# Two attention layers in fp32 on one core: the value products leave PSUM by VectorE instead of ScalarE

## Chip, cores and metric

The kernel runs on one core of one Trainium2 chip. The metric is the device time of one execution in microseconds (us).

## What is computed

The input is four images of 32 x 32 positions and 768 channels, in fp32. Two layers follow each other. Each normalises its input over 32 groups of channels, computes attention over the 1024 positions of an image with 12 heads of 64 channels and a relative position bias in both directions, projects the result and adds it to the layer's input. Cut to what matters here:

```
qkv    = groupnorm(x) @ Wqkv (+ qkv_b, in layer 1 only)
scores = scale * q @ k.T + rel_h[..., :, None] + rel_w[..., None, :]
attn   = softmax(scores)
out    = attn @ v                      # the value products
x      = x + (out @ Wproj + bproj)
```

The bias of the values can be added after the softmax, because the weights of one query sum to one. The kernel does this: in layer 1 the step that takes the value products out of PSUM adds the values' part of `qkv_b`.

## The kernel before

There are eight images in the sense of the code (`images`): four in layer 0, then the same four in layer 1. An image has six pairs of heads (`pair`), so there are 48 groups `g`, and each group has eight units `n` of 128 queries (`units`). The order of all instructions is written out by hand in the main loop, and each engine works through its own queue in that order.

In unit (g, n) the loop issues, in this order:

- on GpSimd, the position biases of the unit after next (`biases`, L429);
- on TensorE, the scores of the next unit (`scores`, L443) into two PSUM tiles `s`; on VectorE, the sum of scores and bias with its row minimum (L455), and on ScalarE the exponentials (L459) (`exponentials`);
- at n = 7, on TensorE, the position products of the next group (`positions`, L381) into a PSUM tile `tp`, which ScalarE copies out (L386, L389); at n = 2 another half of them;
- parts of the projections of other groups (`products`, tile `pj`; `project_values`, tile `pv`; `project_out_two`, tile `oo`), whose matmuls are recorded at L285 and L313. Such a group of matmuls is split in two halves. Between the halves VectorE rewrites one column of a weight tile with its own value (L274, `between`), so that the second half waits for it;
- on VectorE, the transpose of the unit's weights (`turn`, L479) into a tile `tb`, of which there are two; then a DMA writes `tb` to a scratch tensor `td` in DRAM, and another one reads it back in the order that the value products need, into `pt` (L490);
- the division of the next unit's weights by their sums (`divide`): a reciprocal on VectorE (L467), and two multiplications on ScalarE (L473), one of which is on GpSimd (L471) where n is 2 or 4;
- at n = 6 the value products of the first two quarters of the group's queries, and at n = 2 those of the last two quarters of the group before (`weigh`, L508): 64 matmul records into one PSUM tile `av` of 128 x 512, followed by one instruction that writes it to the tile `attn` in SBUF (L517 in layer 0, a plain copy; L519 in layer 1, a copy with the bias `bqkv`). The last group's last two quarters are done apart, in two instructions of 128 x 256.

The tiles `tp`, `pj`, `pv`, `oo`, `o` and `av` share one PSUM pool, `ps_m`, with two buffers. The next of them can start on TensorE only when the buffer that it gets has been read out:

```
ps_s = ctx.enter_context(tc.tile_pool(name="ps_s", bufs=2, space=PSUM))
ps_m = ctx.enter_context(tc.tile_pool(name="ps_m", bufs=2, space=PSUM))
```

At the change from n = 6 to n = 7, one of the two buffers holds the half-finished group `oo` and the other one holds `av`. What TensorE has next after the scores is `tp`, which gets the buffer of `av`.

The image's normalisation is prepared while the image before is still worked on: its statistics and their square root in pair 3, and its application on ScalarE (L233, `apply`) in pair 4.

Of the kernel before, what the change touches and what calls it, by code (L numbers as in the profile page):

```python
# [32 lines left out]
AF = mybir.ActivationFunctionType  # L33
ALU = mybir.AluOpType
# [22 lines left out]
def attention_blocks(ctx: ExitStack, tc: tile.TileContext, a: dict, out: bass.AP):  # L57
    nc = tc.nc
# [115 lines left out]
    bqkv = const.tile([P, 3, NP], FP, tag="bqkv", name="bqkv")  # L174
# [320 lines left out]
    def weigh(g, quarters):  # L495

        if quarters[0] == 0:  # L500
            attn_of[g] = apool.tile([P, S], FP, tag="attn", name=f"attn_{g}")
        n = len(quarters)
        av = ps_m.tile([P, S], FP, tag="m", name=f"av_{g}_{quarters[0]}")[:, : n * 2 * P]
        for at, quarter in enumerate(quarters):
            for k in range(NT):
                for h in range(2):
                    rows = slice(h * D, (h + 1) * D)
                    nc.tensor.matmul(  # L508
                        av[rows, at * 2 * P : (at + 1) * 2 * P], lhsT=v_of[g][:, k, rows],
                        rhs=pt_of[g, quarter].rearrange("p n r k h i -> p (n r) k h i")[:, :, k, h, :],  # L510
                        start=(k == 0), stop=(k == NT - 1),
                    )
        at = quarters[0] * 2 * P
        to = attn_of[g][:, at : at + n * 2 * P]
        im, pair = divmod(g, NP)
        if images[im][0] == 0:
            nc.scalar.copy(to, av)  # L517
        else:
            nc.scalar.activation(to, av, AF.Identity, bias=bqkv[:, 2, pair : pair + 1])  # L519

    def cuts(im):
        return [0, NC // 2, NC] if im + 1 < NI else [0, NC // 2, NC - 1, NC]
# [161 lines left out]
    with tc.manual_schedule(engines=ENGINES):  # L684
# [55 lines left out]
        for at, (g, n) in enumerate(units):  # L740
            im, pair = divmod(g, NP)
# [81 lines left out]
            if n == 6:  # L823
                weigh(g, (0, 1))
            elif n == 2 and g:
                weigh(g - 1, (2, 3))
# [4 lines left out]
        for quarter in (2, 3):  # L831
            weigh(NPAIR - 1, (quarter,))
# [57 lines left out]
```

## Time and profile before

| what | value |
|---|---|
| median of 3 runs | 3404.13 us (3402.43 to 3408.83) |
| the profiled execution | 3401.86 us |
| its span | 3400.0 us |
| TensorE matmul busy | 3324.9 us, 98% of the span |
| VectorE busy | 2347.4 us, 69% |
| ScalarE busy | 2090.8 us, 61% |
| GpSimd busy | 2332.3 us, 69% |
| granted TensorE clock | 0.998 |

The span runs from the first to the last instruction of the program. PE is TensorE's matmuls, PEld its weight loads, DVE VectorE, ACT ScalarE, POOL GpSimd and SP the engine that issues most DMAs. L443 is line 443 of the kernel. In a row of waits, the part ahead of the arrow waited for the part behind it; the numbers are the total time in us, how often, and the longest one. In a timeline, a row has start and duration in us, engine, line, operation, output and inputs, how many instructions were merged, and in brackets the idle time of the engine before it and what ended it.

### The profile page before, as it was taken

What the parts mean: (1) busy time and instruction counts of PE and PEld (TensorE: products, weight loads), DVE (VectorE), ACT (ScalarE), POOL (GpSimd) and SP (SyncE); (2) the same over time, 40 slices, a digit from 0 to 9 for tenths busy, and PEclk for the clock granted to TensorE, in tenths of its full rate; (3) what the DMA queues carried; (4) which work ended last, traced back from release to release, by engine and by line L of the source; (5) the groups of instructions that cost most, each with busy time, mean ns of one, the idle gap of its engine ahead of it and who ended that gap; (6) DMA issues with size and microseconds to landing.
All of it is one profiled execution on the core that took longest, in us unless ns stands there. A gap on an engine that the chain in (4) does not pass through costs nothing.

```text
span 3400.0 us, 58086 instructions
## 1 busy us (share of the span) xinstructions
PE 3324.9 (98%) x21600; PEld 1877.2 (55%) x21600; DVE 2347.4 (69%) x3826; ACT 2090.8 (61%) x3237; POOL 2332.3 (69%) x1184
## 2 busy tenths in 40 slices
PE   6999999999999999999999999999999999999998
PEld 3555555555555555555555555555555555555554
DVE  3776677766777666766767766666766676666675
ACT  2666756566566666566665666666666667665663
POOL 5776866668666686666866668666686667766662
PEclk9999999999999999999999999999999999999999
DMA  3898989999998998889888989989988999898887
GB/s 112 307 325 300 335 298 337 321 304 327 317 318 316 318 324 309 309 297 332 313 309 311 312 311 320 317 310 315 325 314 305 332 299 335 308 311 301 312 292 259
DMA packets 534777, 1046.97 MB, mean 308 GB/s; under 512 B 149728, under 2 KB 212704, under 8 KB 485344
## 3 DMA queue, kind: packets, MB, share of 16 engines
q1 hardware_dynamic: 479936, 1015.84, 85.3%
q10 hardware_dynamic: 54560, 27.43, 2.8%
q8 instruction: 171, 2.80, 0.3%
q14 instruction: 110, 0.90, 0.1%
HBM read 568.01 MB, written 475.10 MB: 307 GB/s over the span
## 4 chain that ended last, share of the span: by engine, by line
PE 81%; DMA 7%; DVE 4%; ACT 4%; issue 2%; POOL 1%; SPq 1%; ACTq 0%; DVEq 0%; POOLq 0%
PE pj L285 20%; PE s L443 16%; PE av L508 14%; PE pv L285 13%; PE oo L285 12%; DMA td<-tb 5%; PE pj L313 3%; PE tp L381 2%; DVE tb L479 2%; ACT sc L473 2%; POOL sc L429 1%; PE o L587 1%; ACT sc L459 1%; DMA xn<-in_x 1%; ACT xn L233 1%
## 5 line engine op out<-in xcount | busy, mean ns | idle before, releaser
L429 POOL TENSOR_TENSOR sc<-rel 128x1024 f32<-128x1024 f32 x768 | 1879.7, 2476 | 660.1 <-DVE tb L479 626.8
L455 DVE CUSTOM_DVE_ANT_0 sc<-s,sc 128x1024 f32<-128x1024 f32 x768 | 910.8, 1225 | 747.9 <-PE s L443 561.9
L459 ACT ACTIVATE sc<-sc,sm 128x1024 f32<-128x1024 f32 x768 | 878.7, 1146 | 472.0 <-DVE sm L455 471.0
L473 ACT ACTIVATE sc<-sc,sm 128x1024 f32<-128x1024 f32 x674 | 743.0, 1143 | 581.2 <-DVE sm L467 415.4
L479 DVE STREAM_TRANSPOSE tb<-sc 128x1024 f32<-128x1024 f32 x768 | 909.9, 1227 | 52.8 <-DMA td<-tb 44.7
L443 PE MATMUL s<-k,q 64*128 64x512 f32 x3072 | 738.3, 596 | 1.7 <-DVE sm L455 1.7
L508 PE MATMUL av<-pt,v 128*64 128x256 f32 x6144 | 685.5, 381 | 7.0 <-DMA pt<-td 6.0
L508 PEld LDWEIGHTS av<-pt,v 128*64 128x64 f32 x6144 | 434.8, 137 | 287.0 <-issue 45.0
L285 PE MATMUL pv<-wv,xn 64*128 64x256 f32 x4608 | 522.8, 376 | 1.0 <-DVE wv L274 1.0
L285 PEld LDWEIGHTS pv<-wv,xn 64*128 64x128 f32 x4608 | 447.3, 187 | 114.1 <-issue 56.9
L285 PE MATMUL oo<-attn,wo 64*128 64x512 f32 x2112 | 477.1, 591 | 0.0
L443 PEld LDWEIGHTS s<-k,q 64*128 64x128 f32 x3072 | 290.1, 187 | 313.7 <-issue 292.2
L285 PEld LDWEIGHTS oo<-attn,wo 64*128 64x128 f32 x2112 | 202.0, 188 | 228.7 <-issue 227.2
L471 POOL TENSOR_SCALAR sc<-sc,sm 128x1024 f32<-128x1024 f32 x94 | 105.1, 1118 | 311.8 <-DVE sm L467 310.8
L285 PE MATMUL pj<-xn,wa 64*128 64x512 f32 x1152 | 269.1, 598 | 33.2 <-DVE xn L235 27.4
L285 PE MATMUL pj<-xn,w 64*128 64x512 f32 x1152 | 263.4, 589 | 1.6 <-DVE w L274 1.6
L285 PE MATMUL pj<-s,w 64*128 64x512 f32 x576 | 262.7, 589 | 1.5 <-ACT attn L519 0.8
L285 PE MATMUL pj<-s,wc 64*128 64x512 f32 x576 | 262.8, 589 | 0.0
L285 PEld LDWEIGHTS pj<-xn,wa 64*128 64x128 f32 x1152 | 113.6, 189 | 168.9 <-issue 127.4
L285 PEld LDWEIGHTS pj<-xn,w 64*128 64x128 f32 x1152 | 112.4, 187 | 136.6 <-issue 134.1
L404 ACT COPY rel<-raw 32x256 f32<-32x256 f32 x384 | 155.1, 404 | 22.2 <-DMA part<-res 6.7
L285 PEld LDWEIGHTS pj<-s,wc 64*128 64x128 f32 x576 | 107.4, 187 | 67.0 <-issue 67.0
(68 smaller groups left out, 2111.4 us busy)
## 6 DMA issues: line engine op xcount, KB each, us to landing
td<-tb SPq DMA_DIRECT2D x384, 1024.0 KB, 6.5
pt<-td SPq DMA_DIRECT2D x382, 1024.0 KB, 8.9
tdr<-t ACTq DMA_DIRECT2D x96, 256.0 KB, 6.3
part<-res SPq DMA_DIRECT2D x84, 256.0 KB, 4.5
res<-part SPq DMA_DIRECT2D x84, 256.0 KB, 4.9
wa<-in_wqk SPq DMA_DIRECT2D x48, 384.0 KB, 3.2
wc<-in_wqk SPq DMA_DIRECT2D x48, 384.0 KB, 7.4
wv<-in_wv SPq DMA_DIRECT2D x24, 768.0 KB, 12.2
```

The source lines that it names most:

```text
L285: nc.tensor.matmul(to, lhsT=w, rhs=x, start=(half, at) == (0, 0), stop=(half, at) == (1, n - 1))
L313: nc.tensor.matmul(t[:, h, :], lhsT=w[rows, c, :], rhs=x[c][rows, :], start=(c == 0), stop=(c == NB - 1),)
L381: nc.tensor.matmul(ps[:, h, j, :], lhsT=q[rows, at * P : (at + 1) * P], rhs=tabs[l][rows, :], start=True, stop=True,)
L404: nc.scalar.copy(rel[rows, :, 0, :, :], raw[rows, :, :, WIDE - 1 - HW - y : WIDE - 1 - y])
L429: nc.gpsimd.tensor_tensor(sc.rearrange("p (a k) (u l) -> p a (k u) l", a=4, l=8), rel[:, h, 0, m, :].unsqueeze(1).unsqueeze(3).to_broadcas ...
L443: nc.tensor.matmul(ps[h][:, cols], lhsT=q[rows, n * P : (n + 1) * P], rhs=k[rows, cols], start=True, stop=True,)
L455: nc.vector.tensor_tensor_reduce(out=sc, in0=ps[h], in1=sc, scale=-scale, scalar=BIG, op0=ALU.add, op1=ALU.min, accum_out=st[:, 0, h : h + 1],
L459: nc.scalar.activation(sc, sc, AF.Exp, bias=st[:, 0, h : h + 1], scale=-1.0, accum_out=st[:, 1, h : h + 1],)
L471: nc.gpsimd.tensor_scalar(sc, sc, st[:, 2, h : h + 1], 1.0, ALU.mult, ALU.mult)
L473: nc.scalar.mul(sc, sc, st[:, 2, h : h + 1])
L479: nc.vector.transpose(tb[:, :, h, :], sc_of[g, n, h])
L508: nc.tensor.matmul(av[rows, at * 2 * P : (at + 1) * 2 * P], lhsT=v_of[g][:, k, rows], rhs=pt_of[g, quarter].rearrange("p n r k h i -> p (n ...
```

## The change

The instruction that takes `av` out of PSUM goes from ScalarE to VectorE, with the same tiles and at the same place in the written order. In layer 0 it is a copy; in layer 1 it is a VectorE operation with one tensor input and one bias value per partition. There are 97 such instructions in the program (48 copies of 128 x 512, 47 with the bias of 128 x 512, and two with the bias of 128 x 256). The instructions of TensorE, GpSimd and SP and their order stay as they are.

```
@@ -514,9 +514,9 @@
         to = attn_of[g][:, at : at + n * 2 * P]
         im, pair = divmod(g, NP)
         if images[im][0] == 0:
-            nc.scalar.copy(to, av)
+            nc.vector.tensor_copy(to, av)
         else:
-            nc.scalar.activation(to, av, AF.Identity, bias=bqkv[:, 2, pair : pair + 1])
+            nc.vector.tensor_scalar(to, av, bqkv[:, 2, pair : pair + 1], None, ALU.add)
```

More of the change, by code (lines that the diff above doesn't have):

```diff
@@ L516, in weigh @@
         if images[im][0] == 0:
-            nc.scalar.copy(to, av)
+            nc.vector.tensor_copy(to, av)
         else:
-            nc.scalar.activation(to, av, AF.Identity, bias=bqkv[:, 2, pair : pair + 1])
+            nc.vector.tensor_scalar(to, av, bqkv[:, 2, pair : pair + 1], None, ALU.add)
     def cuts(im):
```

## Prediction

> **What bounds the kernel now.** I read the page's busy line first. It says TensorE, and says how little is left to win:
>
> ```profile
> PE 3324.9 (98%) x21600; PEld 1877.2 (55%) x21600; DVE 2347.4 (69%) x3826; ACT 2090.8 (61%) x3237; POOL 2332.3 (69%) x1184
> ```
>
> So the question is not how busy VectorE and ScalarE are, but where TensorE is idle: 3400.0 - 3324.9 = 75 us. The table of windows puts 27 us before 37 us (the start), 13 us up to 300, 12 us in the last 102 us, and 22.7 us in the long middle:
>
> ```profile
> 300.00:3298.00 2998.00, 2975.34 (x19536) 1.00 0.90 315
> ```
>
> (columns: window, its length, PE busy, granted clock, DMA share, GB/s). The view of waits, for PE alone, names what ends this idle time:
>
> ```profile
> PE pj L285 <- DVE xn L235: 27.4, 1, 27.4
> PE tp L381 <- ACT attn L517: 13.0, 12, 2.0
> PE tp L381 <- ACT attn L519: 7.3, 8, 2.1
> PE av L508 <- DMA pt<-td: 6.0, 6, 1.6
> PE o L587 <- ACT attn L519: 3.8, 3, 2.0
> ```
>
> The first row is the start. The next two are 20 waits, 20.3 us, and the reader is to see what they wait for: the very instruction that the change moves. `tp` needs the PSUM buffer of `av`, and TensorE stands until ScalarE has read it out.
>
> The timeline of one such place (group 27, unit 6 to 7), ScalarE's and VectorE's rows, tells why ScalarE is late:
>
> ```profile
> 1976.67 2.37 DVE L479 STREAM_TRANSPOSE tb<-sc 128x1024 f32<-128x1024 f32 x2 [3.21 <-DMA td<-tb]
> 1978.97 0.12 DVE L467 RECIPROCAL sm<-sm 128x2 f32<-128x2 f32 x1
> 1979.01 0.13 DVE L274 TENSOR_REDUCE wo<-wo 128x1 f32<-128x1 f32 x1
> 1979.99 1.22 DVE L455 CUSTOM_DVE_ANT_0 sc<-s,sc 128x1024 f32<-128x1024 f32 x1 [0.85 <-PE s L443]
> ```
> ```profile
> 1979.12 2.19 ACT L473 ACTIVATE sc<-sc,sm 128x1024 f32<-128x1024 f32 x2 [3.45 <-DVE wo L274]
> 1981.22 0.67 ACT L519 ACTIVATE attn<-av,bqkv 128x512 f32<-128x512 f32 x1
> ```
> ```profile
> 1977.86 1.99 PE L443 MATMUL s<-k,q 64*128 64x512 f32 x8
> 1981.94 0.83 PE L381 MATMUL tp<-tab,q 64*128 64x128 f32 x10 [2.09 <-ACT attn L519]
> ```
>
> `av` was complete at 1977.93. ScalarE reads it at 1981.22, because the two divisions stand ahead of it, and these wait for VectorE's reciprocal, which is late because the transposes waited for a DMA. VectorE itself idles 0.85 us before L455.
>
> [...] The trace's nearest rows agree as lower neighbours: 684 (L608, a sum of PSUM and SBUF, 128x512) and 747 ns (L606, the same with a bias). [...] So L429 on GpSimd should keep its 2476 ns; no row of before shows this instruction. [...] the rows above agree, since L519 starts right behind the divisions.
>
> **The change part by part.**
>
> *Removed from ScalarE:* 48 x 562 ns + 47 x 666 ns + 2 x 473 ns = 59 us. ScalarE is 39% idle and only its lateness counts, so this alone is worth nothing; L459 behind it starts up to 0.6 us earlier.
>
> *Added to VectorE:* 97 instructions. [...] from above 759 (L331, PSUM with bias and an SBUF input); I take 690, so 66 us, 71% busy in place of 69%. In the new order the eviction stands directly behind the next unit's reciprocal and ahead of L274 and L455. It waits for the end of `av`, so at what times do its neighbours run? I measured from the end of `av` in VectorE's timeline, at all places. L455 starts at +2.06 (2.04 at n = 2), held by the scores that TensorE does after `av`. The reciprocal ends at -2.21 at n = 2 nearly always. At n = 6 it ends at -2 to -1 in most groups without a stall, and between -0.7 and +0.65 in those with one, but for two with +1.13 and +1.16. The eviction therefore lies between max(0, reciprocal) + 0.05 and about 0.75 us later: it fits in VectorE's idle time ahead of L455. Cost on the path: nothing, hidden by the wait for the scores. Were that cover gone, 0.69 us at each of 95 places.
>
> *The stall at `tp`.* Undisturbed, `tp` starts 1.82 us after the first scores matmul (2258.21 to 2260.03); at 1977.86 it took 4.08. I summed the excess over 1.82 in all 47 groups: 23.7 us in 20 groups (0.4 to 2.3 each), 14 of them in pair 3 or 4. `tp` could start at `av` + 1.75. With the eviction ending at max(0, reciprocal) + 0.75, 18 of the 20 end by +1.40 and stall no more; the other two end at +1.9 and keep 0.2 each. Gain 23.7 - 0.4 = **23.3 us**.
>
> *Two more stalls of the kind*, `pj` at n = 3 in groups 5 and 40 (352.65 and 2853.38), where ScalarE applied the norm ahead of the eviction (+4.5 us): 0.9 each, gain **1.8 us**.
>
> *The end.* In the last group `o` waits 2.2 us at 3357.93 for an eviction at 3357.31, whose reciprocal had ended at 3355.10: with VectorE it ends near 3355.85 and **2.0 us** are won. A like wait of 1.3 us at 3329.98 is followed by waits for `pt`; I count nothing.
>
> *The wait added to VectorE.* At n = 3 L274 on `wv` (`between`) now stands behind the eviction, and the second half of `pv` waits for it. L274 ends at about +0.05 + 0.69 + 0.15 = +0.9; the first weight load of that half starts at +1.33 (2019.87). Margin 0.4 us. In groups 6 and 12 a BN_STATS of 0.68 us lies between them: loss 2 x 0.3 = **0.6 us**. SP's and GpSimd's queues are not passed by anything.
>
> *What is late next.* `pt`. The second quarter's data land 2.6 us (median) before their first matmul, but in stalled groups often only 1 us. Taking the stall of a group from the next group's margin leaves at least 0.2 us everywhere, so no wait is new in a first count. But DMA is at 0.90 of the middle window, and all of this pushes it to 2698 / 2974 = 0.91. Given back: 0 to 10 us; I take **2.5**.
>
> Sum: 23.3 + 1.8 + 2.0 - 0.6 - 2.5 = 24 us. The profiled execution of 3401.86 would become 3377.9. It lies 2.3 us under the median of the runs, 3404.13; that median less 24 is **3380**.
>
> **The rivals.** (A) *The stall turns into waits for DMA.* Lateness starts with transposes waiting for `tb` (44.7 us in 26 waits on VectorE), a DMA matter, and TensorE running earlier doesn't make DMA faster. For it: the 0.90, and six waits for `pt` that exist already. Against: groups without a stall all take 68.72 us, so DMA keeps up with a TensorE that never waits. Half to two thirds given back: 3404 - 11 = 3393.
> (B) *The change doesn't do what it says:* the buffer is not what holds `tp`, the releaser being inferred. Against: `tp` starts 0.04 to 0.05 us after ScalarE's eviction at each place that I read. No change: 3404.
> (C) *Slower: VectorE's queue holds TensorE.* With the eviction ahead of L274 and L455, a longer one delays `pv` at n = 3. The margin of 0.4 us is used up at 1.1 us of eviction; to outweigh the 27 us won, 34 us / 47 groups = 0.72 us more, that is 1.8 us an eviction. No row of 128x512 on VectorE from PSUM comes near (the slowest, strided, 1225 ns), and L274's own place is not on the path otherwise. It would give 3411.
>
> **How the numbers follow.** About 0.2% (7 us) is what a measurement of this kernel can tell from no change. My forecast has 0.73; A 0.16, of which some 0.04 ends within 0.2%; B 0.05; C 0.06. Faster: 0.73 + 0.12 = 0.85; same 0.09; slower 0.06. The range: nothing given back and the 1.3 us at the end won too is 29 us, 3375, less 3 us for the scatter of three medians; at the other end A's 3393. I give 3372 to 3394.
>
> **What would show it.** In the profile after: the rows of `tp` waiting for `attn` gone or under 1 us in all; PE idle in the middle window down from 22.7 to about 3 us; the eviction on VectorE at 0.65 to 0.76 us; L455 still at +2.06; DVE 71%, ACT 60%. The prediction is wrong if `tp` still waits (for whom, the waits tell), if PE's waits for `pt` or `wv` grow by over 10 us, or if L429 gets slower.

## The result, and the profile after

The changed kernel takes 3369.21 us in the median of four runs (3366.87 to 3373.25), the kernel before in the same set 3405.31 us (3402.43 to 3408.83): 36 us less, a ratio of 0.9898 with a 95% interval from 0.9886 to 0.9911. The prediction named 3380 us and a range of 3372 to 3394; direction and mechanism hold, the gain is larger than forecast, and the time lies 3 us under the range. Two more sets of runs of the same two kernels, made with the experiments, give 3400.09 to 3373.87 (ratio 0.993, 0.9916 to 0.9943) and 3401.18 to 3371.59 (0.991, 0.9897 to 0.9923). The gain of the three sets is 36, 26 and 30 us.

The profiled execution after took 3373.25 us, with a span of 3370.8. Busy line and the window of the middle, as they stood in the prediction:

```profile
PE 3319.2 (98%) x21600; PEld 1875.8 (56%) x21600; DVE 2415.5 (72%) x3923; ACT 2039.6 (61%) x3140; POOL 2332.4 (69%) x1184
```
```profile
300.00:3268.00 2968.00, 2966.27 (x19514) 1.00 0.91 318
```

The share of 98% says nothing new. The window does: TensorE idles 1.7 us in 2968, where it idled 22.7 in 2998. VectorE took over 68 us of work and ScalarE gave up 51. The new instruction itself, as the view of `attn` has it (shortest, median and longest in ns):

```profile
L519 DVE TENSOR_SCALAR attn<-av,bqkv x49: 483/751/752, 1754.9 to 3360.7; 128x512 f32<-128x512 f32 x47, 128x256 f32<-128x256 f32 x2
L517 DVE COPY attn<-av x48: 664/691/693, 127.6 to 1722.7; 128x512 f32<-128x512 f32 x48
```

The view of waits for PE no longer has a row in which `tp` waits for `attn`:

```profile
PE pj L285 <- DVE xn L235: 26.7, 1, 26.7
PE av L508 <- DMA pt<-td: 9.0, 6, 2.6
PE pj L285 <- DVE wa L274: 3.8, 2, 3.2
...
PE o L587 <- DVE attn L519: 0.6, 1, 0.6
```

The waits for `pt`, the weights that a DMA reads back for the value products, grew from 6.0 to 9.0 us. The timeline of the same place as before, group 27 at the change from unit 6 to 7, first VectorE, then ScalarE, then TensorE:

```profile
1959.50 2.37 DVE L479 STREAM_TRANSPOSE tb<-sc 128x1024 f32<-128x1024 f32 x2 [2.54 <-DMA td<-tb]
1961.79 0.12 DVE L467 RECIPROCAL sm<-sm 128x2 f32<-128x2 f32 x1
1961.84 0.73 DVE L519 TENSOR_SCALAR attn<-av,bqkv 128x512 f32<-128x512 f32 x1
1962.48 0.14 DVE L274 TENSOR_REDUCE wo<-wo 128x1 f32<-128x1 f32 x1
1963.08 1.23 DVE L455 CUSTOM_DVE_ANT_0 sc<-s,sc 128x1024 f32<-128x1024 f32 x1 [0.46 <-PE s L443]
```
```profile
1961.95 2.19 ACT L473 ACTIVATE sc<-sc,sm 128x1024 f32<-128x1024 f32 x2 [2.79 <-DVE sm L467]
```
```profile
1960.95 1.99 PE L443 MATMUL s<-k,q 64*128 64x512 f32 x8
1962.77 1.06 PE L381 MATMUL tp<-tab,q 64*128 64x128 f32 x16
```

The reader is to see three things. The transposes are late as before, because a DMA still holds `tb` (2.54 us of idle time here). The eviction now runs (from 1961.84) while ScalarE only begins its divisions (1961.95). And `tp` starts 1.82 us after the scores, the undisturbed distance; L455 still waits for the scores after the eviction (0.46 us).

### The profile page after: what moved, and what is told of

It reads as the page before. It is cut to its first block, busy times and chain, and to the rows that moved or that the text cites. A ratio compares the mean times of both kernels' runs of the same rounds, so it can differ in the third digit from the quotient of the medians.

```text
span 3370.8 us, 58086 instructions
## 1 busy us (share of the span) xinstructions
PE 3319.2 (98%) x21600; PEld 1875.8 (56%) x21600; DVE 2415.5 (72%) x3923; ACT 2039.6 (61%) x3140; POOL 2332.4 (69%) x1184
## 4 chain that ended last, share of the span: by engine, by line
PE 93%; DMA 4%; DVE 2%; issue 1%; ACT 0%; SPq 0%; POOL 0%; ACTq 0%; DVEq 0%
PE pj L285 21%; PE av L508 19%; PE s L443 19%; PE pv L285 15%; PE oo L285 13%; PE pj L313 3%; PE tp L381 3%; DMA td<-tb 2%; DMA pt<-td 1%; PE o L587 1%; DVE tb L479 1%; DMA xn<-in_x 0%; DVE sc L455 0%; DVE st L188 0%; DMA per<-mv 0%
## 5 line engine op out<-in xcount | busy, mean ns | idle before, releaser
L429 POOL TENSOR_TENSOR sc<-rel 128x1024 f32<-128x1024 f32 x768 | 1880.3, 2478 | 636.8 <-DVE tb L479 601.6
L455 DVE CUSTOM_DVE_ANT_0 sc<-s,sc 128x1024 f32<-128x1024 f32 x768 | 910.9, 1225 | 524.0 <-PE s L443 459.5
```

The source lines that it names most:

```text
L429: nc.gpsimd.tensor_tensor(sc.rearrange("p (a k) (u l) -> p a (k u) l", a=4, l=8), rel[:, h, 0, m, :].unsqueeze(1).unsqueeze(3).to_broadcas ...
L455: nc.vector.tensor_tensor_reduce(out=sc, in0=ps[h], in1=sc, scale=-scale, scalar=BIG, op0=ALU.add, op1=ALU.min, accum_out=st[:, 0, h : h + 1],
```

## The experiments

**The changed kernel again**, to size the gain.

> The changed kernel once more, against the kernel before, to size the gain. The first profiles give 28.6 us (3401.86 to 3373.25), the first medians 36.1. If the two profiled executions were ordinary ones, more rounds give 28 to 30 us. If the profiled execution of before was a lucky one and that of after an unlucky one (they were the lowest and the highest of their kind), more rounds give 33 to 37 us, and the new profile's span is some 5 us below 3370.8, with fewer waits of TensorE for pt (9.0 us in the first).

Measured: 3373.87 us (3370.95 to 3380.64) against 3400.09 (3392.33 to 3412.39, 19 runs), 26 us. Beside the third set:

> The changed kernel in a third set of runs, beside the kernels of this set. The two sets so far give 36 and 26 us of gain. If that is scatter between executions, the third lies between 24 and 38 and its profile again shows under 3 us of waits at tp.

Measured: 3371.59 us (3369.13 to 3371.61) against 3401.18, 30 us. The excess at `tp`, summed as in the prediction, is 0.6, 2.4 and 0.3 us in the three profiles, and PE's waits for `pt` are 9.0, 3.8 and 7.4 us. The second set's 26 us lie in neither range of its expectation (28 to 30, or 33 to 37), though the waits for `pt` did become fewer, and the new span, 3368.6, is 2.2 us below the first, not 5. The third set's 30 us lie in the range expected. The three intervals don't all overlap, so what differs from set to set is more than the scatter inside a set; its cause was not found.

**The kernel before again.**

> The kernel before in another profiled execution, to see how much its stalls scatter. If its time scatters because of them (its runs lie between 3392 and 3412 us), the sum of excess at tp differs from 23.7 by several us, or the half-clock stretches and the waits for pt do.

Measured: 3402.82 us. The excess at `tp` is 22.8 us (23.8 in the first profile), so this term is stable. What differs is the clock. After three of the stalls TensorE's granted clock was half for 3.4 us; in the first profile this followed one stall in the middle and one at the end. The windows around one of them, PE alone (columns: window, its length, busy, granted clock, DMA share, GB/s):

```profile
2464.00:2467.00 3.00, 1.64 (x8) 1.00 0.93 367
2468.00:2471.00 3.00, 3.00 (x20) 0.52 0.94 308
2472.00:2475.00 3.00, 3.00 (x16) 1.00 0.97 316
```

The stall of 1.98 us ends at 2467.6, and the clock is 0.52 in the window right after it.

**ScalarE first.** The eviction stays on ScalarE, ahead of the divisions:

```
             turn(g, n)
             run_part(1 if n == 0 else len(pieces))
+            if n == 6:
+                weigh(g, (0, 1))
+            elif n == 2 and g:
+                weigh(g - 1, (2, 3))
             if at + 1 < len(units):
                 divide(*units[at + 1])
...
-            if n == 6:
-                weigh(g, (0, 1))
-            elif n == 2 and g:
-                weigh(g - 1, (2, 3))
```

> The eviction stays on ScalarE, but is issued ahead of the two divisions instead of behind them; no other engine's order changes. Theory 1 (place in the queue): what counts is that the buffer of av is read out before tp needs it; the eviction ends near av + 0.75 or reciprocal + 0.6, tp waits under 1 us in all, and the time is that of the changed kernel within 5 us. Theory 2 (the engine): ScalarE's relief of 59 us or VectorE's free time makes the gain; ScalarE keeps its load here and the divisions now wait for av, so under half of the gain, 3390 us or more.

Measured: 3369.56 us, ratio 0.9914 (0.99 to 0.9928); in the third set 3369.76, ratio 0.9907 (0.9893 to 0.992). ScalarE and TensorE at the same place of the main loop:

```profile
1956.65 0.69 ACT L519 ACTIVATE attn<-av,bqkv 128x512 f32<-128x512 f32 x1 [1.89 <-PE av L508]
1957.35 2.19 ACT L473 ACTIVATE sc<-sc,sm 128x1024 f32<-128x1024 f32 x2
1959.46 0.59 ACT L386 COPY t<-tp 128x512 f32<-128x512 f32 x1
```
```profile
1956.54 1.99 PE L443 MATMUL s<-k,q 64*128 64x512 f32 x8
1958.36 1.06 PE L381 MATMUL tp<-tab,q 64*128 64x128 f32 x16
```

ScalarE now waits for `av` (1.89 us here), evicts, and divides after that; `tp` loses 0.04 us in the whole run. TensorE's matmuls stand in the same order as before. With no instruction moved to another engine the gain is the same. So it is the place in the queue that counts, and not the engine. Set directly beside the changed kernel:

> ScalarE's eviction ahead of the divisions once more, to place it against the changed kernel. If it is really better, because its eviction doesn't wait for VectorE's reciprocal (tp loses 0.04 us in its first profile, 2.4 in the changed kernel's second), it is 2 to 5 us faster; if the 4 us of the first set were scatter, within 2 us of it.

It is 4.3 and 1.8 us faster in the two medians, and the runs of the two overlap (3367.93 to 3371.38 against 3369.13 to 3371.61 in the third set). This version is at least as good, and spares VectorE the 68 us.

**ScalarE's load given back.** The changed kernel, with one line more behind the eviction:

```
             nc.vector.tensor_scalar(to, av, bqkv[:, 2, pair : pair + 1], None, ALU.add)
+        nc.scalar.copy(to, to)
```

> The changed kernel with an additional copy of attn onto itself on ScalarE, at the old place behind the divisions: the PSUM buffer is released by VectorE, but ScalarE has its load of before, and attn itself is ready as late as before. Theory 1 (release of the buffer): within 4 us of the changed kernel. Theory 2 (ScalarE's relief, or attn being ready earlier for oo): back to 3390 us or more.

Measured: 3372.41 us (3371.53 to 3373.55), 0.8 us above the changed kernel of the same set. ScalarE's busy time is back at 2094.1 us (before 2090.8). ScalarE's relief, and `attn` being ready sooner, are worth nothing that can be measured.

**One half of the change alone.** The eviction goes to VectorE only where `quarters[0] == 0` (n = 6), or only where it is greater (n = 2 and the end):

```
+        if quarters[0] == 0 and images[im][0] == 0:
+            nc.vector.tensor_copy(to, av)
+        elif quarters[0] == 0:
+            nc.vector.tensor_scalar(to, av, bqkv[:, 2, pair : pair + 1], None, ALU.add)
-        if images[im][0] == 0:
+        elif images[im][0] == 0:
             nc.scalar.copy(to, av)
```

> Only the eviction at n = 6 goes to VectorE (48 of 97), the one at n = 2 and those of the last group's end stay on ScalarE. Theory 1: nearly all of the gain, since 20 of the 22 stalls in the middle are at n = 6: the changed kernel's time plus 1.8 us (pj at n = 3 in pair 4) plus up to 3.5 us at the end, so 2 to 6 us above it. Theory 2: half of the gain, about 18 us above it.

> Only the evictions at n = 2 and at the end go to VectorE (49 of 97). Theory 1: TensorE keeps its waits at tp (20 to 24 us); 2 to 6 us below the kernel before. Theory 2: half of the gain, about 18 us below it.

Measured: n = 6 alone 3383.56 us, 17 us below the kernel before (ratio 0.9952, 0.9937 to 0.9967) and 10 above the changed kernel, more than the 2 to 6 expected; n = 2 alone 3398.9 us, 1 us below the kernel before (0.9992, 0.9981 to 1.0003), not to be told from nothing. With n = 2 alone the waits of PE at `tp` stay:

```profile
PE tp L381 <- ACT attn L521: 14.8, 13, 2.0
PE tp L381 <- ACT attn L523: 8.0, 7, 1.9
```

The waits of PE with n = 6 alone show where the rest went:

```profile
PE av L508 <- DMA pt<-td: 8.8, 7, 2.1
PE pj L285 <- ACT attn L521: 5.5, 4, 2.6
PE pj L285 <- ACT attn L523: 4.7, 3, 2.4
```

(In both kernels L521 and L523 are the two forms of the eviction left on ScalarE.) In the profile before, `pj` lost at n = 3 in pair 4 in two of seven images, 1.8 us. With n = 6 relieved, it loses in all seven, 11.4 us more than in the changed kernel. A likely reason, not tested by itself, is that the stall at n = 6 had let ScalarE catch up. The two halves are worth 17 and 1 us by themselves and 26 together: the second one pays only once the first is done.

**Longer evictions.** The changed kernel, with the eviction to VectorE done twice, by one line more, or three times, by two such lines:

```
         im, pair = divmod(g, NP)
+        nc.vector.tensor_copy(to, av)
         if images[im][0] == 0:
```

> The changed kernel with the eviction done twice on VectorE, so some 0.69 us are added at each of 95 places (66 us of work). By the prediction's margin (the second half of pv needs L274 by av + 1.33, and L274 now ends at +1.6) it costs 0.25 us in 46 groups at n = 3, 12 us, and about 2.4 us at tp: 14 us slower than the changed kernel. If the margin is really that of the first matmul (+1.75), pv loses nothing and it is 2 to 4 us slower. Were VectorE's busy time as such what counts, it would be 66 us slower.

> The changed kernel with the eviction done three times on VectorE, 2.1 us in all: the rival C of the prediction made real. The buffer of av is free at +2.15, tp needs it at +1.75: 0.4 us in 47 groups, 19 us, and some 5 us more where the reciprocal is late. L274 ends at +2.3: by a margin of +1.33 pv loses 0.95 us in 46 groups (44 us), 68 us slower than the changed kernel; by a margin of +1.75 it loses 0.55 us (25 us), some 50 us slower. Both put it slower than the kernel before, by 15 to 40 us.

Twice: 3376.06 us (3369.76 to 3380.74), 4.5 us above the changed kernel of the set, near the 2 to 4 expected of the wider margin and far from 14 or 66. PE's waits hold 1.8 us at `tp`, and 1.5 at `pv`, of which 1.0 stands in the changed kernel too. The profiled execution was the fastest of the six (3369.76), so it does not show where the 4.5 us go. Three times: 3435.56 us (3435.02 to 3436.24), 33 us slower than the kernel before, ratio 1.0098 (1.0077 to 1.0119). Its waits for PE:

```profile
PE tp L381 <- DVE wo L274: 22.0, 42, 1.5
PE pv L285 <- DVE wv L274: 21.3, 47, 1.0
```

Both rows name L274, the instruction behind the eviction in VectorE's queue. For `pv` that is right: it starts 0.05 us after L274's end. For `tp` it is the last eviction: `tp` starts 0.15 us after its end in all 44 places, also in the two where a BN_STATS, and not L274, comes next. From start to start against the changed kernel of the third set, `tp` loses 29.9 us in 44 places and `pv` 28.0 in 46. This is rival C made real, on both of its places: the cover ends between 1.4 and 2.1 us of eviction. The margin of the prediction, +1.33 us at `pv`, is wrong: with two evictions L274 ends at +1.5 or +1.6 after the end of `av` and costs nothing; only in groups 6 and 12, where a BN_STATS lies between, it ends at +2.1, and `pv` loses 0.42 us in each. The margin is that of the first matmul, near +1.75.

**One division less ahead of ScalarE's eviction.** The kernel before, with one word changed in `divide`:

```
-            if h == 0 and n in (2, 4) and not last:
+            if h == 0 and n in (2, 4, 7) and not last:
```

> The kernel before, with the first of the two divisions that stand ahead of the n = 6 eviction done by GpSimd, as it is for n = 2 and 4: ScalarE reaches the eviction 1.05 us earlier. Theory 1 (the eviction's place in ScalarE's queue): each stall at tp shrinks by up to 1.05 us, 18.8 of 23.7 us by the list of stalls of the profile before, and the time falls by 15 to 20 us, if GpSimd's 1.1 us more don't hold up its biases. Theory 2 (the engine): ScalarE's 50 us less would make about the same, but the stalls at tp would shrink evenly, and not down to a rest of 5 us in the groups with over 1.05.

Measured: 3382.94 us, 19 us below the kernel before (ratio 0.9947, 0.9927 to 0.9966). The waits of PE at `tp`, 20.3 us before:

```profile
PE tp L381 <- ACT attn L517: 5.0, 6, 1.2
PE tp L381 <- ACT attn L519: 0.5, 1, 0.5
```

The excess at `tp` falls to 8.0 us: by 15.7, where the list of stalls less 1.05 us each says 18.8. Of the seven stalls under 1.05 us five are at 0.1 or less; of the 13 longer ones all but one are shorter, though not each by 1.05. So a smaller relief of the same wait gives a smaller gain, with the eviction still on ScalarE and behind one division; the 3 us missing were not traced.

## Why the prediction was right, and where it was too low

*The stall at `tp`*: 23.3 us were predicted. From start to start of TensorE's matmuls, whose order is the same in both programs, the two profiles give 23.2. Right, and shown by ScalarE's eviction ahead of the divisions, by the half at n = 6, and by the division on GpSimd.

*The eviction on VectorE* was priced at 690 ns, my estimate; the median of the copy is 691, that of the form with the bias 751. Against the nearest rows before, 684 ns (L608) and 747 ns (L606, with a bias), they took 7 and 4 ns longer. It hid as forecast: L455 starts at +2.06, the eviction ends at +0.74 or +0.80 where the reciprocal is early. GpSimd's L429 kept its time (2476 to 2478 ns), which no row of before could show. ScalarE's relief of 59 us was a sum of durations; its busy time fell by 51, because 95 of the 97 evictions began before the instruction ahead of them on ScalarE had ended (by 0.09 us in the rows of group 27). Nothing on the path hung on that.

*Where the profile's sum is off.* Until the first eviction of group 3 the two profiles differ by 0.7 us, in the middle by 27.6, at the end by 0.9; together the 29.2 us of the spans. I had 22.0 for the middle (23.3 + 1.8 - 0.6 - 2.5) and 2.0 for the end. The step that failed is the term of the stall, which I took as its waiting time alone:

- The stall also holds up the weight load ahead of `tp`. Undisturbed, that load starts 0.1 to 0.43 us before the first matmul (0.42 us at 2260.03). Where it starts together with that matmul, the second pair of matmuls comes 0.104 us late: behind all 20 stalls and in one more place before (1910.4), in five places after. So 16 places are won, 1.7 us.
- TensorE ran at half its clock after some stalls. In the first profile before this happened once in the middle, behind the longest stall (2.26 us at 1981.94), and stretched four steps of `oo` by 0.42 us each, 1.7 us:

```profile
1983.40:1986.70 3.30, 3.30 (x10) 0.50 0.98 355
```

- Two smaller terms were too high. Given back to `pt` in the middle: 1.0 us in place of 2.5. The loss of 0.6 us at `pv` behind BN_STATS did not occur, since the margin was wider.

These make the 5.6 us of the middle: 1.7 + 1.7 + 1.5 + 0.6 = 5.5. At the end 3.5 us won at `o` were mostly spent again: 1.5 us on a later start of scores, and 1.1 us on a wait for `pt` at 3323, behind which TensorE ran at half clock.

*From the profile to the median.* 28.6 us between the profiled executions, 36 between the medians of the first set. The profiled execution before was below all three runs then shown, and the profiled one after was the slowest of its four. I named the first of these gaps (2.3 us) and allowed 3 us for scatter beyond a largest gain of 29 us; that gain lacked the two terms of the stall above, and in the sets of runs the gain moves by 10 us. The lower end of the range was therefore too high. Of the 12 us between the sum of 24 and the first set's 36, the profiles account for 5; the other 7 were not traced. With the second set's median, 3373.87, the time would lie inside the range, so part of the miss is a matter of the set.

*The rivals.* A (given back to DMA) is excluded in its size: the waits for `pt` grew by 3.0 us in the first profile, in the second they were 2.2 below before, in the third 1.4 above. B fell when the rows of `tp` waiting for `attn` were gone. C is true of an eviction three times as long, and not of this one.

## What to carry to other kernels

When an engine that bounds the kernel waits for a buffer, look at what stands ahead of the releasing instruction in its queue, before thinking of which engine is less busy: here an eviction of 0.67 us stood behind two divisions (2.19 us) that it had nothing to do with, and moving it ahead on its own engine gained as much as moving it to another (3369.76 and 3371.59 us in the third set). Here a stall cost more than its waiting time (0.104 us for a late weight load, and in places 1.7 us of clock), and undoing it laid open the next one, at `pj` with n = 6 alone: undo one, and count again what comes late.

## What the hardware showed that I had not expected

TensorE's half-clock stretches in the course of the kernel, all 3.4 us long or twice that, go with idle times of TensorE of some 2 us or more. In the three executions profiled without a relief at n = 6, six of the seven stretches after the start and before the end of the span stand directly behind a stall of 1.9 us or more at `tp` or `o` (1981.9, 3357.9; 726.8, 1563.0, 2467.6; 1841.8), and the seventh, at 3354, begins in one. But five of the twelve such stalls were not followed by one, that of 1.96 us at 1564.7 in the first profile among them.

What tells them apart can be read from the traces. In each of the 13, the half-clock stretches begin on one grid with a step of 3.413 us. Cut along that grid, the stall at 1981.9 has 1.98 of its 2.09 us of idle time in one cell, and the cell behind it is at half clock; the stall at 1564.7 is split into 0.80 and 1.16 us, and no cell is:

```profile
1979.95:1983.36 3.41, 1.42 (x18) 1.00 1.04 291
1983.36:1986.78 3.42, 3.42 (x12) 0.50 0.96 347
```
```profile
1560.12:1563.53 3.41, 2.60 (x16) 1.00 0.74 296
1563.53:1566.95 3.42, 2.27 (x22) 1.00 0.93 247
1566.95:1570.36 3.41, 3.41 (x18) 1.00 1.04 395
```

After the first 100 us the 13 traces have 12488 whole cells. The ten with 1.97 us or more of idle time were all followed by half clock; of two with 1.89 one was; of the others, all with 1.82 or less, none. (In the first profiles of the two kernels: 1923 cells, of which the four with 1.98 us or more were followed by half clock, and none of the others, at 1.57 or less.) The grid is shifted from execution to execution: in the three profiles of the changed kernel the first stretch begins at 74.35, 74.09 and 73.92 us. So it is in part luck whether a stall of this length costs another 1.7 us. No experiment set an idle time by itself, so the traces show that the two go together, and no more.
